# A fused attention and mixture-of-experts kernel: attention's transposes done together, as 64-row halves

## The chip, the cores and the metric

The kernel runs on one core of a Trainium2 chip. A core has a matrix engine (PE, with its weight loads shown apart as PEld), a vector engine (DVE), a scalar engine (ACT), a general engine (POOL) and a queue for transfers (SP). Each engine works through its own instructions in order, and waits on semaphores for the others. In this kernel PE's results go to PSUM tiles, which DVE and ACT read; the text calls 512 float32 of a partition there a bank, the unit in which the program lays these tiles out. The metric is the device time of one launch in microseconds (us), as the median of several runs. Before the change it is 994.02 us (three runs, 993.91 to 994.19).

## The reference

Inputs are x, 16 blocks of 128 tokens by 512 features, and a context of 16 blocks of 128 by 128. There are two residual layers, all in float32:

```
x = x + attention(layernorm(x), context, context)
        # 32 query heads of 16, 8 key/value heads; softmax(q k^T / 4) v per block of 128 tokens
x = x + moe(layernorm(x))
        # gate: sigmoid(x gate_weight^T); 8 groups of 4 experts, best 4 groups, best 8 experts
        # of 32; weights normalized and times 2.5
        # routed: sum over the 8 experts of w2(silu(x w1^T) * (x w3^T)), inner size 256
        # plus one shared expert of the same shape for all tokens
```

## The kernel before

The kernel has three stretches: attention with the gate's inputs (0 to about 134 us), routing with the shared expert (to about 227 us), and the 32 experts (to the end). The program is in order on PE, DVE, ACT and POOL: the order of the calls is the order of the instructions.

**Attention** (`attention_small`) runs over 32 items (b, i): row block b of 128 tokens, and i, which of each pair of key heads. A loop over steps n = 0 to 31 works on three items at once. In step n PE does, in this order: `scores(n)` (L429: four 32-row matmuls side by side, into two PSUM tiles of two banks each, that every step uses again); `values(n-1)` (L445: four matmuls of 32 output columns side by side, into the tile oT); in some steps `gate_parts`, the gate's partial logits; in even steps `queries(n/2+1)`, four 128 by 128 transposes of the normalized rows xq into the tile tr (L416); in some steps `gate_sums` (L505); `added(n-2)`, four transposes of the attention output into the tile o (L461); and in some steps `gate_turn(b)`, four transposes of the rows of the second layernorm into tr (L227).

The other engines follow. ACT takes the two exponentials of `scores` (L439, `p<-sc`) and copies turned rows to xnT (L228). DVE copies oT to oTs (L454) and the turned queries to qT (L420), and for each item takes a reciprocal of the sums (`ri`, L465) and scales the heads (`at`, L467). POOL adds `at` to the residual rows x (L474). Two further chains run through these queues:

- layernorm: DVE's `layernorm_stats` of a block (L91, L92; `mv1` for the first layernorm, `mv2` for the second, which needs both of the block's adds), then `layernorm_rstd`, a chain of 14 small instructions (L98 to L115), on POOL for most groups of blocks (`first_rstd`, `second_rstd`), then `rows_of` (xq, L394, DVE) or `gate_rows` (xn, L217, POOL; it also stores the rows with a transfer on SP). The tile xn has three buffers.
- keys and values: POOL masks the next four blocks' keys (`keys`, kz, L350, two instructions) and copies their values (`values_of`, L357).

Two tables, `head` and `tail`, say which of these are issued at the beginning and at the end of each step; they set the order on DVE and POOL around the adds. Before, in order of the steps: keys 2 at 9; `second_rstd` at 11, 19, 23, 27 (blocks 0-3, 4-7, 8-9, 10-11) and 30 (12-13); `gate_rows` at 13 to 16, 21 to 24, 25, 26, 29, 30; `first_rstd` of blocks 12 to 15 at 16; keys 3 at 17; `mv2` statistics of block b at the end of step 2b + 4, from 4 to 26; squares of the keys (ACT) and their sums (DVE, `kn`) at 17 to 20. Turned rows are in steps 15 to 18, 23 to 28, 30 and 31. Blocks 12 to 15 are done after the loop, between pieces of the shared expert (`filler`).

The program's PSUM tiles in attention take eight banks: four for scores, and one each for tr, lg (the gate), oT and o.

**Experts.** Rows are gathered in slices of 128 (138 in all, L1360), turned on PE by `turn` (up to four slices at a time, each as eight half transposes of 64 rows, two row groups side by side, L1381), and copied to xnT by ACT and DVE in turn (`turned`, L1397 and L1404). All four slices share one PSUM tile of four banks; a slice's two halves lie in two banks, which slices 0 and 1, and slices 2 and 3, share. `up` (L1429) and `down` (L1483) are the experts' matmuls.

Of the kernel before, what the change touches and what calls it, by code (L numbers as in the profile page):

```python
# [18 lines left out]
P = 128  # L19
EPS = 1e-5  # L20
HD = 16
G = 4
# [24 lines left out]
def tile_xattn_moe(  # L47
# [175 lines left out]
    def gate_turn(b, pool, tag="tr", copy=nc.scalar.copy):  # L223
        xn = xn2.pop(b)
        tr = pool.tile([P, ND, P], F32, tag=tag, name="tr")
        for k in range(ND):
            nc.tensor.transpose(tr[:, k, :], xn[:, ts(k, P)], ident)  # L227
        copy(xnT[b // 4][:, :, ts(b % 4, P)], tr)  # L228
# [43 lines left out]
    def attention_small():  # L272


        with ExitStack() as ph:
# [4 lines left out]
            ps_tr = ph.enter_context(tc.tile_pool(name="ps_tr", bufs=1, space=PSUM))  # L280
            ps_lg = ph.enter_context(tc.tile_pool(name="ps_lg", bufs=1, space=PSUM))
            ps_oT = ph.enter_context(tc.tile_pool(name="ps_oT", bufs=1, space=PSUM))
            ps_o = ph.enter_context(tc.tile_pool(name="ps_o", bufs=1, space=PSUM))
# [37 lines left out]
            warm = ps_o.tile([P, P], F32, tag="o", name="warm")  # L321
# [88 lines left out]

            def queries(b):

                xn = xqs.pop(b)
                tr = ps_tr.tile([P, G, P], F32, tag="tr", name="tr")
                for g in range(G):
                    nc.tensor.transpose(  # L416
                        tr[:, g, :], xn[:, g].rearrange("p k d -> p (k d)"), ident
                    )
                qT = ap2.tile([P, G, P], F32, tag="qT", name="qT")
                nc.vector.tensor_copy(qT, tr)  # L420
                qTs[b] = qT

            def scores(b, i):
                scs = [
                    ps_sc.tile([P, 2, G, P], F32, tag="sc", name="sc") for _ in range(NJ // 2)
                ]
                for j in range(NJ):
# [4 lines left out]
                        rhs=qTs[b][rows],  # L432
# [4 lines left out]
                for j, sc in enumerate(scs):  # L437
                    p = pp.tile([P, 2, G, P], F32, tag="p", name="p")
# [3 lines left out]
            def values(b, i):  # L442
                oT = ps_oT.tile([P, G, P], F32, tag="oT", name="oT")
# [10 lines left out]
                nc.vector.tensor_copy(t, oT)  # L454
                oTs[b, i] = t

            def added(b, i):
                t = oTs.pop((b, i))
                o = ps_o.tile([P, G, NJ, HP], F32, tag="o", name="o")
                for g in range(G):  # L460
                    nc.tensor.transpose(  # L461
                        o[:, g].rearrange("p j e -> p (j e)"), t[:, g, :], ident
                    )
                ri = ap2.tile([P, G, NJ], F32, tag="ri", name="ri")
                nc.vector.reciprocal(ri, o[:, :, :, HD])  # L465
                at = ap2.tile([P, G, NJ, HD], F32, tag="at", name="at")
# [3 lines left out]
                    ri.unsqueeze(3).to_broadcast([P, G, NJ, HD]),  # L470
                    ALU.mult,
                )
                part = xs[b].rearrange("p (j i g d) -> p i g j d", i=2, g=G, d=HD)[:, i]
                nc.gpsimd.tensor_tensor(part, part, at, ALU.add)  # L474

# [75 lines left out]

            turned, parts, sums = {}, {}, {}
            at_head(4, fold_of)
            step = 0
            for first, n in ((0, 4), (4, 4), (8, 2), (10, 2)):
                for b in range(first, first + n):
                    at_tail(2 * b + 4, layernorm_stats, b, mv2)
                done = 2 * (first + n - 1) + 4
                at_head(done + 1, second_rstd, first, n, nc.gpsimd)
                for b in range(first, first + n):  # L560
                    step = max(step + 1, done + 3)
                    at_head(step, gate_rows, b, nc.gpsimd)
                    turned[step + (2 if b < 10 else 1)] = b
                    if b % 2 and b < 10:
                        parts[step + 3], sums[step + 4] = b - 1, b - 1
# [5 lines left out]
            queries(0)  # L571
            keep_warm(FILL[-1])
            for n in range(N):
# [4 lines left out]
                if n == 1:  # L578
                    queries(1)
# [1037 lines left out]
```

## Time and profile before

| | |
|---|---|
| median of the runs | 994.02 us |
| the profiled execution's own time | 1000.94 us |
| its span, from the first to the last instruction | 998.9 us |
| granted PE clock, mean | 0.993 |
| busy: PE, PEld, DVE, ACT, POOL | 976.1, 555.6, 300.3, 286.0, 508.5 us |
| scores of step 0 start; step 31 ends | 9.63 us; 119.76 us |
| last matmul of the gate (L505) starts | 133.26 us |
| first gathered slice turned (L1381) | 227.16 us |

Times inside the profiled execution count from the start of its span. A timeline line gives start, length, engine, source line, operation, what is written from what, shapes, how many are merged, and in brackets how long the engine stood idle before and what released it. "PE busy" holds modelled ends, so a wait shorter than a matmul's length may not show as idle. A line of busy times by stretch gives the stretch, its length, and for each engine its busy time and, in brackets, the number of instructions; then the PE clock granted, the share of the transfer engines, and GB/s.

### The profile page before, as it was taken

What the parts mean: (1) busy time and instruction counts of PE and PEld (TensorE: products, weight loads), DVE (VectorE), ACT (ScalarE), POOL (GpSimd) and SP (SyncE); (2) the same over time, 40 slices, a digit from 0 to 9 for tenths busy, and PEclk for the clock granted to TensorE, in tenths of its full rate; (3) what the DMA queues carried; (4) which work ended last, traced back from release to release, by engine and by line L of the source; (5) the groups of instructions that cost most, each with busy time, mean ns of one, the idle gap of its engine ahead of it and who ended that gap; (6) DMA issues with size and microseconds to landing.
All of it is one profiled execution on the core that took longest, in us unless ns stands there. A gap on an engine that the chain in (4) does not pass through costs nothing.

```text
span 998.9 us, 13416 instructions
## 1 busy us (share of the span) xinstructions
PE 976.1 (98%) x4729; PEld 555.6 (56%) x4729; DVE 300.3 (30%) x984; ACT 286.0 (29%) x443; POOL 508.5 (51%) x659
## 2 busy tenths in 40 slices
PE   9999999998999999999999999999999999999996
PEld 5344444546666556676666666667654444444453
DVE  7787678961211112111112111111111111211110
ACT  5567622411222222222222222222222222221221
POOL 3788733752445536444546454545464444455443
PEclk9999999998999999999999999999999999999998
DMA  9011105133767657667767676777576777677543
GB/s 316 4 44 43 63 24 197 46 117 118 171 136 168 142 128 184 150 146 181 162 147 164 155 161 155 161 166 182 131 172 150 150 176 185 141 158 170 116 67 45
DMA packets 59867, 137.12 MB, mean 137 GB/s; under 512 B 12168, under 2 KB 16392, under 8 KB 59792
## 3 DMA queue, kind: packets, MB, share of 16 engines
q0 software_dynamic: 32032, 69.25, 37.0%
q1 hardware_dynamic: 27680, 66.81, 19.9%
q8 instruction: 39, 0.64, 0.3%
q14 instruction: 36, 0.29, 0.1%
q10 hardware_dynamic: 80, 0.13, 0.0%
HBM read 96.71 MB, written 46.73 MB: 144 GB/s over the span
## 4 chain that ended last, share of the span: by engine, by line
PE 77%; POOL 9%; issue 5%; DVE 4%; DMA 2%; another core or an unknown queue 1%; ACT 0%; POOLq 0%; DVEq 0%; ACTq 0%
PE gu L1429 43%; PE y L1483 21%; PE gu L253 5%; PE trx L1381 4%; POOL out_dram L1455 2%; DMA out_dram<-yw,token 2%; POOL xn L217 2%; PE y L1279 1%; POOL x L474 1%; DVE st L91 1%; PE tok L946 1%; POOL kz L350 1%; DVE oTs L454 1%; POOL h L113 0%
## 5 line engine op out<-in xcount | busy, mean ns | idle before, releaser
L1429 PE MATMUL gu<-xnT,wup 128*128 128x256 f32 (+27 forms) x1664 | 493.6, 447 | 4.4 <-DVE xnT L1397 4.4
L1429 PEld LDWEIGHTS gu<-xnT,wup 128*128 128x128 f32 x1664 | 316.4, 191 | 197.9 <-issue 133.5
L1455 POOL DMA_INDIRECT out_dram<-yw,token x150 | 234.7, 1565 | 352.5 <-ACT yw L1492 241.2
L1483 PE MATMUL y<-wdn,sa 128*128 128x512 f32 (+2 forms) x672 | 263.5, 599 | 0.1
L1440 DVE TENSOR_TENSOR sa<-sl,gu 128x256 f32<-128x256 f32 (+27 forms) x104 | 52.2, 502 | 561.9 <-PE gu L1429 519.1
L1360 POOL DMA_INDIRECT xg<-rows,token x138 | 141.9, 1028 | 49.9 <-issue 33.1
L1492 ACT ACTIVATE yw<-y,wt 128x512 f32<-128x512 f32 x138 | 95.0, 688 | 197.7 <-PE y L1483 193.7
L1483 PEld LDWEIGHTS y<-wdn,sa 128*128 128x128 f32 (+2 forms) x672 | 97.9, 170 | 95.1 <-issue 84.6
L1438 ACT ACTIVATE sl<-gu 128x256 f32<-128x256 f32 (+27 forms) x104 | 46.7, 449 | 233.3 <-PE gu L1429 226.9
L1397 ACT COPY xnT<-trx 128x512 f32<-128x512 f32 x65 | 38.1, 586 | 158.4 <-PE trx L1381 67.9
L439 ACT ACTIVATE p<-sc 128x1024 f32<-128x1024 f32 x64 | 62.1, 1022 | 30.2 <-PE sc L429 30.2
L1397 DVE COPY xnT<-trx 128x512 f32<-128x512 f32 x61 | 42.2, 691 | 65.7 <-issue 33.2
L253 PE MATMUL gu<-xnT,sup 128*128 128x512 f32 x128 | 59.2, 601 | 0.7 <-ACT ssl L261 0.7
L940 POOL TENSOR_SCALAR hq<-slice_q,sq 128x138 f16<-128x138 f16 x32 | 35.2, 1114 | 34.7 <-DVE sq L1245 18.5
L1381 PEld LDWEIGHTS trx<-ident,xg 64*128 64x128 f32 x1104 | 37.2, 139 | 17.8 <-issue 17.5
L1381 PE MATMUL trx<-ident,xg 64*128 64x64 f32 x1104 | 42.1, 226 | 0.0
L429 PE MATMUL sc<-qT,kz 32*128 32x512 f32 x256 | 41.5, 639 | 0.2 <-ACT p L439 0.2
L474 POOL TENSOR_TENSOR x<-x,at 128x256 f32<-128x256 f32 x32 | 23.4, 733 | 26.3 <-DVE at L467 26.3
L445 PE MATMUL oT<-p,va 128*32 128x512 f32 x256 | 34.1, 605 | 2.5 <-DVE oTs L454 2.5
L253 PEld LDWEIGHTS gu<-xnT,sup 128*128 128x128 f32 x128 | 22.8, 190 | 24.1 <-issue 21.5
L1412 DVE SCALAR_TENSOR_TENSOR own<-expert,owner,xg 128x32 f32<-128x32 f32 x138 | 31.5, 245 | 0.0
L1279 PE MATMUL y<-sdn,sa 128*128 128x512 f32 x64 | 29.3, 595 | 0.0
(180 smaller groups left out, 494.0 us busy)
## 6 DMA issues: line engine op xcount, KB each, us to landing
wup<-in_w_dram SPq DMA_DIRECT2D x64, 512.0 KB
wdn<-in_w_dram SPq DMA_DIRECT2D x32, 512.0 KB
rows<-xn SPq DMA_DIRECT2D x16, 256.0 KB
out_dram<-x SPq DMA_DIRECT2D x16, 256.0 KB
x<-in_x_dram SPq DMA_DIRECT2D x15, 256.0 KB
out_dram<-yw,token POOLq DMA_INDIRECT x150
xg<-rows,token POOLq DMA_INDIRECT x138
cTs<-in_cT_dram SPq DMA_DIRECT2D x4, 256.0 KB
```

What stands on the lines that cost most here:

```text
L253: nc.tensor.matmul(acc, lhsT=sup[:, w, d, ts(i, P)], rhs=xnT[k][:, d, :], start=(d == 0), stop=(d == ND - 1),)
L429: nc.tensor.matmul(scs[j // 2][:, j % 2], lhsT=kzs[b // 4 % 2][rows, b % 4, i, :], rhs=qTs[b][rows], start=True, stop=True, tile_position= ...
L439: nc.scalar.activation(p, sc, AF.Exp, scale=1.0 / HD**0.5)
L1360: nc.gpsimd.indirect_dma_start(out=t, out_offset=None, in_=rows[:, :], in_offset=bass.IndirectOffsetOnAxis(ap=token[:, j : j + 1], axis=0) ...
L1381: nc.tensor.matmul(tr[:, h, s, d, :], lhsT=xg[j][rows_of_half, ts(d, P)], rhs=ident[rows_of_half, rows_of_half], start=True, stop=True, is ...
L1397: copy(xnT[n % NTB][:, :, col : col + P].rearrange("p d (h t) -> p h d t", h=2), tr)
L1429: nc.tensor.matmul(acc[:, 0:m], lhsT=wup[k % NW][:, w, d, ts(i, P)], rhs=xnT[n % NTB][:, d, 0:m], start=(d == 0), stop=(d == ND - 1),)
L1438: nc.scalar.activation(banks[2][:, 0:m], acc[:, 0:m], AF.Silu)
L1440: nc.vector.tensor_tensor(acts[n % NTB][:, i, 0:m], banks[2][:, 0:m], acc[:, 0:m], ALU.mult)
L1455: ins = nc.gpsimd.indirect_dma_start(out=flat, out_offset=bass.IndirectOffsetOnAxis(ap=token2[:, k - 1 : k] if a else token[0:b, j : j + 1 ...
L1483: nc.tensor.matmul(y[c0:c1, :], lhsT=acts[n % NTB][:, i, col : col + c1 - c0], rhs=wdn[pieces[n][0] % NW][:, i, :], start=(i == 0), stop=( ...
L1492: nc.scalar.activation(yws[j], y, AF.Copy, scale=wt[:, j : j + 1])
```

## The change

In attention, the sets of four 128-row transposes of one step (queries, added heads, turned rows) are issued one after the other by a new function `transposes`, at the place in the step where queries stood, behind `gate_parts` and ahead of `gate_sums`. Each 128 by 128 transpose becomes two of 64 rows in PE's two row groups: eight half transposes a set. A step has at most two sets. They go into one PSUM tile x of two banks, one bank for each row group, both sets in both banks; only when all have been issued do the readers follow (qT, then `ri` and `at`, then the copy of the turned rows, which stays on ACT). The tiles tr and o go, so x has their two banks. The layouts of qT, oTs, `at` and the residual add change with the halves.

The order of the gate's work changes: `second_rstd` of blocks 0-2, 3-5, 6-8, 9-11 at steps 9, 15, 21, 27; `gate_rows` at 10, 12, 14 and so on to 26 for blocks 0 to 8, then 28, 29, 30; turned rows three steps later, in odd steps 13 to 29, then 30 and 31, and block 11 after the loop; `gate_parts` at 16, 20, 24, 28 and 31. Blocks 12 to 15 and the last heads are still turned as full transposes, in a tile with the same tag.

In the experts, `turn` uses two PSUM tiles of two slices each instead of one of four (the same four banks); ACT copies the first two slices and DVE the last two.

```diff
-    def gate_turn(b, pool, tag="tr", copy=nc.scalar.copy):
+    def gate_turn(b, tr, copy=nc.scalar.copy):
         xn = xn2.pop(b)
-        tr = pool.tile([P, ND, P], F32, tag=tag, name="tr")
         for k in range(ND):
             nc.tensor.transpose(tr[:, k, :], xn[:, ts(k, P)], ident)
         copy(xnT[b // 4][:, :, ts(b % 4, P)], tr)
...
-            ps_tr = ph.enter_context(tc.tile_pool(name="ps_tr", bufs=1, space=PSUM))
+            ps_x = ph.enter_context(tc.tile_pool(name="ps_x", bufs=1, space=PSUM))
             ps_lg = ph.enter_context(tc.tile_pool(name="ps_lg", bufs=1, space=PSUM))
             ps_oT = ph.enter_context(tc.tile_pool(name="ps_oT", bufs=1, space=PSUM))
-            ps_o = ph.enter_context(tc.tile_pool(name="ps_o", bufs=1, space=PSUM))
...
+            H = P // 2
+            halves = [slice(h * H, (h + 1) * H) for h in range(2)]
+            def transposes(*sets):
+                x = ps_x.tile([P, 2, 2, 2, P], F32, tag="x", name="x")
+                for s, (of, split, _) in enumerate(sets):
+                    for k in range(4):
+                        for h, rows in enumerate(halves):
+                            if split:
+                                to = x[:, h, :, s, ts(k, P // 4)]
+                                by = ident[rows, rows].rearrange("p (a b) -> p a b", a=2)
+                            else:
+                                to = x[:, h, k // 2, s, ts(k % 2, H)]
+                                by = ident[rows, rows]
+                            nc.tensor.matmul(
+                                to,
+                                lhsT=of[rows, k, :],
+                                rhs=by,
+                                start=True,
+                                stop=True,
+                                is_transpose=True,
+                                tile_position=(h * H, 0),
+                            )
+                for s, (_, _, then) in enumerate(sets):
+                    then(x[:, :, :, s])
             def queries(b):
-                xn = xqs.pop(b)
-                tr = ps_tr.tile([P, G, P], F32, tag="tr", name="tr")
-                for g in range(G):
-                    nc.tensor.transpose(
-                        tr[:, g, :], xn[:, g].rearrange("p k d -> p (k d)"), ident
-                    )
-                qT = ap2.tile([P, G, P], F32, tag="qT", name="qT")
-                nc.vector.tensor_copy(qT, tr)
-                qTs[b] = qT
+                xn = xqs.pop(b).rearrange("p g k d -> p g (k d)")
+                def then(x):
+                    qTs[b] = ap2.tile([P, 2, 2, P], F32, tag="qT", name="qT")
+                    nc.vector.tensor_copy(qTs[b], x)
+                return xn, False, then
...
+                nc.vector.tensor_copy(
+                    t.rearrange("p g (h s) -> p h g s", h=2),
+                    oT.rearrange("p (h g s) -> p h g s", h=2, g=G),
+                )
                 oTs[b, i] = t
...
-            def added(b, i):
-                t = oTs.pop((b, i))
-                o = ps_o.tile([P, G, NJ, HP], F32, tag="o", name="o")
-                for g in range(G):
-                    nc.tensor.transpose(
-                        o[:, g].rearrange("p j e -> p (j e)"), t[:, g, :], ident
-                    )
-                ri = ap2.tile([P, G, NJ], F32, tag="ri", name="ri")
+            def add(b, i, o):
+                ri = ap2.tile([P, NJ, G], F32, tag="ri", name="ri")
                 nc.vector.reciprocal(ri, o[:, :, :, HD])
-                at = ap2.tile([P, G, NJ, HD], F32, tag="at", name="at")
+                at = ap2.tile([P, NJ, G, HD], F32, tag="at", name="at")
                 nc.vector.tensor_tensor(
                     at,
                     o[:, :, :, 0:HD],
-                    ri.unsqueeze(3).to_broadcast([P, G, NJ, HD]),
+                    ri.unsqueeze(3).to_broadcast([P, NJ, G, HD]),
                     ALU.mult,
                 )
-                part = xs[b].rearrange("p (j i g d) -> p i g j d", i=2, g=G, d=HD)[:, i]
+                part = xs[b].rearrange("p (j i g d) -> p i j g d", i=2, g=G, d=HD)[:, i]
                 nc.gpsimd.tensor_tensor(part, part, at, ALU.add)
+            def added(b, i):
+                return (
+                    oTs.pop((b, i)),
+                    True,
+                    lambda x: add(b, i, x.rearrange("p h r (g e) -> p (h r) g e", e=HP)),
+                )
+            def turn_of(b):
+                def then(x):
+                    nc.scalar.copy(
+                        xnT[b // 4][:, :, ts(b % 4, P)].rearrange(
+                            "p (r k) (h s) -> p h r k s", r=2, h=2
+                        ),
+                        x.rearrange("p h r (k s) -> p h r k s", k=2),
+                    )
+                return xn2.pop(b).rearrange("p (k d) -> p k d", d=P), False, then
...
-            step = 0
-            for first, n in ((0, 4), (4, 4), (8, 2), (10, 2)):
-                for b in range(first, first + n):
+            for first in range(0, 12, 3):
+                for b in range(first, first + 3):
                     at_tail(2 * b + 4, layernorm_stats, b, mv2)
-                done = 2 * (first + n - 1) + 4
-                at_head(done + 1, second_rstd, first, n, nc.gpsimd)
-                for b in range(first, first + n):
-                    step = max(step + 1, done + 3)
-                    at_head(step, gate_rows, b, nc.gpsimd)
-                    turned[step + (2 if b < 10 else 1)] = b
-                    if b % 2 and b < 10:
-                        parts[step + 3], sums[step + 4] = b - 1, b - 1
+                at_head(2 * first + 9, second_rstd, first, 3, nc.gpsimd)
+            for b in range(11):
+                n = min(2 * b + 13, b + 21)
+                turned[n] = b
+                at_head(max(n - 3, b + 19 if b > 8 else 0), gate_rows, b, nc.gpsimd)
+            at_head(30, gate_rows, 11, nc.gpsimd)
+            for b in range(0, 8, 2):
+                parts[2 * b + 16], sums[2 * b + 17] = b, b
+            parts[31] = 8
             at_tail(28, layernorm_stats, 12, mv2)
...
                 if n > 0:
                     values(*items[n - 1])
                 if n in parts:
                     gate_parts(parts[n])
+                sets = []
                 if n % 2 == 0 and 0 < n // 2 < B - 1:
-                    queries(n // 2 + 1)
+                    sets.append(queries(n // 2 + 1))
+                if n > 1:
+                    sets.append(added(*items[n - 2]))
+                if n in turned:
+                    sets.append(turn_of(turned[n]))
+                if sets:
+                    transposes(*sets)
                 keep_warm(FILL.get(n, 0))
                 if n in sums:
                     gate_sums(sums[n])
-                if n > 1:
-                    added(*items[n - 2])
-                if n in turned:
-                    gate_turn(turned[n], ps_tr)
...
-            added(*items[N - 2])
+            transposes(added(*items[N - 2]), turn_of(11))
             values(*items[N - 1])
+            gate_sums(8)
             gate_rows(13, nc.vector)
-            gate_turn(12, ps_tr)
-            added(*items[N - 1])
-            gate_turn(13, ps_tr)
+            both = ps_x.tile([P, 2, ND, P], F32, tag="x", name="tr")
+            tr, o = both[:, 0], both[:, 1]
+            gate_turn(12, tr)
+            last = oTs.pop(items[N - 1])
+            for g in range(G):
+                nc.tensor.transpose(o[:, g], last[:, g, :], ident)
+            add(*items[N - 1], o.rearrange("p g (j e) -> p j g e", e=HP))
+            gate_turn(13, tr)
...
-        ps_x = ctx.enter_context(tc.tile_pool(name="ps_x", bufs=1, space=PSUM))
+        ps_x = ctx.enter_context(tc.tile_pool(name="ps_x", bufs=2, space=PSUM))
...
-            tr = ps_x.tile([P, 2, NX, ND, H], F32, tag="trx", name="trx")
+            trs = [
+                ps_x.tile([P, 2, 2, ND, H], F32, tag="trx", name="trx")
+                for _ in range(-(-len(js) // 2))
+            ]
...
-                            tr[:, h, s, d, :],
+                            trs[s // 2][:, h, s % 2, d, :],
...
-                turned(j, tr[:, :, s], (nc.scalar.copy, nc.vector.tensor_copy)[s % 2])
+                turned(j, trs[s // 2][:, :, s % 2], (nc.scalar.copy, nc.vector.tensor_copy)[s // 2])
```

## The prediction

> **What bounds the kernel now.** I read the page first (engine shares, slices), then PE's waits, then busy time by stretch, then the timelines of 34 to 62 us and 300 to 306 us.
>
> ```profile
> PE 976.1 (98%) x4729; PEld 555.6 (56%) x4729; DVE 300.3 (30%) x984; ACT 286.0 (29%) x443; POOL 508.5 (51%) x659
> PE gu L1429 <- DVE xnT L1397: 4.4, 1, 4.4
> ```
>
> PE fills 98% of the span; from 232 us on (the experts) its one long wait is 4.4 us at the first expert. Only attention, up to about 134 us, can give or lose much. By stretch (us, then busy PE, PEld, DVE, ACT, POOL):
>
> ```profile
> 35.00:55.00 20.00, 18.84 (x134) 7.49 (x132) 15.14 (x36) 11.56 (x12) 14.75 (x38) 1.00 0.01 2
> 55.00:75.00 20.00, 18.58 (x148) 8.56 (x144) 16.56 (x38) 13.43 (x19) 16.31 (x25) 1.00 0.15 54
> 75.00:95.00 20.00, 19.52 (x153) 8.69 (x153) 15.23 (x36) 13.89 (x17) 16.60 (x38) 1.00 0.11 41
> ```
>
> PE looks full, but DVE and POOL stand at 75 to 83%, in order, each waiting for the other. The reader is to see that PE's cover is thin. The timeline of POOL, then of DVE, around steps 9 to 11 (start, length):
>
> ```profile
> 42.77 0.72 POOL L474 TENSOR_TENSOR x<-x,at 128x256 f32<-128x256 f32 x1
> 43.47 3.12 POOL L350 TENSOR_SCALAR kz<-cTs,odd 128x512 f32<-128x512 f32 x2
> 46.55 0.73 POOL L474 TENSOR_TENSOR x<-x,at 128x256 f32<-128x256 f32 x1
> 48.61 0.28 POOL L98 TENSOR_SCALAR ve<-mv 128x4 f32<-128x4 f32 x1
> 52.34 0.20 POOL L115 TENSOR_TENSOR rstd<-h,r 128x4 f32<-128x4 f32 x1
> 53.89 2.08 POOL L217 TENSOR_SCALAR xn<-x,mv,rstd 128x512 f32<-128x512 f32 x1
> ```
>
> ```profile
> 46.27 0.42 DVE L467 TENSOR_TENSOR at<-o,ri 128x256 f32<-128x256 f32 x1
> 47.32 0.69 DVE L91 BATCH_NORM_STATS2 st<-x 128x6 f32<-128x512 f32 x1 [0.63 <-POOL x L474]
> 48.15 0.66 DVE L394 TENSOR_SCALAR xq<-x,mv,rstd 128x512 f32<-128x512 f32 x1
> 48.73 0.68 DVE L454 COPY oTs<-oT 128x512 f32<-128x512 f32 x1
> ```
>
> DVE's statistics of row block 3 (47.32) start 0.04 us after POOL's add of step 9 lands (46.55 + 0.73). The rstd chain of the second layernorm (48.61 to 52.54, 3.9 us, step 11) comes after it. Last, transposes in both forms, and the copies behind them:
>
> ```profile
> 50.88 0.66 PE L416 MATMUL tr<-ident,xq 128*128 128x128 f32 x4
> 51.37 0.60 PE L461 MATMUL o<-ident,oTs 128*128 128x128 f32 x4
> 51.90 0.31 PEld L429 LDWEIGHTS sc<-qT,kz 32*128 32x128 f32 x8 [0.17 <-issue]
> 302.41 1.21 PE L1381 MATMUL trx<-ident,xg 64*128 64x64 f32 x32
> 303.67 0.59 ACT L1397 COPY xnT<-trx 128x512 f32<-128x512 f32 x1 [2.24 <-PE trx L1381]
> 304.28 0.69 DVE L1397 COPY xnT<-trx 128x512 f32<-128x512 f32 x1 [1.12 <-issue]
> ```
>
> A set of four full transposes holds PE 0.49 us (50.88 to 51.37). Four sets as halves hold it from 302.41 to 303.55, where the next matmul starts: 0.285 a set. ACT's and DVE's copies from one tile go one after the other.
>
> **1. PE work removed.** 59 sets become halves: 16 of queries, 31 of `added`, 12 of turned rows. In attention the neighbours are 32-row and 32-column matmuls, which no row shows next to halves; bounds 0.25 and 0.49 (no gain), taken 0.30, near the expert row with one entry. So 59 x 0.19 = 11.2 us less PE work. [...]
>
> How much reaches the step? Call S(n) the start of step n's scores; before: S10 41.95, S11 45.60, S12 48.25. Scores take 1.07 us, values 1.00. Both score tiles are reused each step, so the second half of scores(n+1) waits for the second exp(n), which ends 3.2 us after S(n). The row at 45.60 shows it: exps run from 46.83 to 48.77, the held-back half starts at 48.82. Hence a pair of steps costs 3.22 + 1.07 + 1.0 + the transposes of the even step: 5.29 + 1.02 = 6.31, as measured (6.30). With 0.6 for two sets as halves it is 5.9: 0.4 us a pair, not 0.8, since ACT takes over.
>
> Up to step 8 DVE is back to back (33.7 to 38 us) and hides most of it: with the saved transposes on the path (0.3 us by step 2, two shorter sets before S9) S10 comes about 0.9 us early, POOL's add of step 7 0.3 us early.
>
> **2. rstd chain from step 11 to step 9, behind the keys and ahead of step 9's add.** The program as built has on POOL: add 8, kz x2, rstd chain, add 9. POOL is busy without a gap from add 7 on, so add 9 lands at 46.6 - 0.3 + 3.9 + 0.73 = 50.9, not 47.28. DVE's statistics of block 3 wait for it, and behind them in DVE's queue stand xq (0.6), the oT copy (0.68) and step 11's reciprocal and `at`. DVE, free at 46.0, sits idle 4.9 us. PE then waits: values(11) needs oT free, 50.97 + 0.82 + 0.61 + 0.68 = 53.1; plus 1.0 and 0.63, S13 = 54.8 against 51.90, so **+2.9 us**. Of the 4.9 us, 2.0 are PE's own lead there (0.9 at S10, 1.1 that scores and values run ahead).
>
> **3. Steps 13 to 21: more POOL work, and a copy tied to DVE.** Through step 18 the new order puts on POOL one rstd chain (3.9) and one gate-row pass (2.08) more than before. From the statistics of step 14 (63.3) POOL runs rstd 3.9, add 0.7, rstd1 3.9, gate rows 2.1, add 0.7, kz 3.1: add 17 starts at 77.8, against 74.79 before. **+3.0** at 21 steps, no gain from PE. A new wait: added heads and turned rows now share two banks, so ACT's copy of turned rows waits for DVE's `at`; before it started 0.11 us after the transpose. Behind it in ACT's queue stand the next two exps (1.94) and sq. Where DVE is late (steps 13, 15, 19) exps start 0.9 to 2.3 us later than the scores allow; in step 20 to 21 that costs 1.8 us more: S22 about +4.7. Bounds: 0 (DVE early) and 1.3 a turn (DVE row chain 0.68 + 0.25 + 0.42). As to why it must wait: the 303.67 and 304.28 rows show it here. [...]
>
> **4. Steps 22 to 31: the gain.** POOL has slack, and each odd step has one turn instead of bursts. Before, steps 22 to 26 took 18.6 us (83.68 to 102.29): turns of 0.55, gate parts 0.55, sums 0.37, and waits for gate rows (0.59 in step 24). Now steps 22 and 23 cost 5.95, steps 24 and 25 7.0 (with parts 0.43, sums 0.37 and 0.25 for late exps), step 26 2.7: 15.65 us. S27 is at +4.7 - 3.0 = +1.7.
>
> **5. The end.** Before, after step 26's statistics POOL did rstd, add, add, gate rows, add, gate rows, rstd: 104.09 to 120.71, 16.6 us, waits for `at` among them. Now it does rstd 3.9, three gate rows 6.2, three adds 2.1, rstd 3.9 = 16.1 without a gap, from 106.25 (S27 at 104.0, then qT 0.7, reciprocal and `at` 0.7, statistics 0.8). So the last rstd ends at 122.4: **+1.7**, however far PE catches up by then. DVE's gate rows 12 wait for it, and behind them the last heads. In the epilogue the joint set waits for the joint tile, where three tiles stood: turn 12 for ACT's copy of turn 11 behind DVE's `at`, **+0.7** (bounds 0 and 1.3, the chain of part 3).
>
> **6. Experts.** Two tiles let ACT and DVE copy side by side; copies end 1.3 us earlier but PE waits for neither (303.55 to 305.37 is `down`). At the first expert both copies go on ACT: 2 x 0.59 for 0.62 + 0.69: **-0.1**. PE's 11.2 us are covered by nothing here.
>
> Costed at nothing: oT's copy in new order and turned rows' copy (0.69 and 0.59 in that form at L1397), row stores on SP (3.4 us to land, buffer reused two turns later or after its turn). POOL's add has longer runs: 0.73 taken; bounds 0.26 (its memset, 1.02 ns an element) and 1.04 (gate rows, 4.06), some -1.9 to +1.2 on the last chain.
>
> **Sum:** +1.7 + 0.7 - 0.1 = +2.3 us. The profiled execution took 1000.94 (span 998.9): 1003.2 (1001.2). It stands 6.9 above the median, 994.02; carried over unscaled: **996.3**.
>
> **Rivals.** *A, faster:* DVE's backlog of steps 6 to 8 dissolves. POOL sat idle 3.3 us before add 7 (37.92), waiting for `at`; if PE's shorter sets bring that `at` forward by 3.3, add 9 lands near 47.6 and DVE hardly waits. It decides from a lead of some 3 us at add 7 on (I count 0.3). Then the 2.9 are gone and PE keeps its 0.9 of S10 and 0.6 more to S13: -4.4, 991.9; with adds at 0.26, 990. Against it: DVE was back to back there with statistics that don't move. *B, nothing:* ACT's copy costs no exp time (DVE early): -1.8 in step 21 and the same in the end: 994.5. For it: DVE is only 75% busy. *C, worse:* POOL and DVE get in each other's way more: xq took 0.52 to 1.08 us, the slow ones beside gate rows; ten slow ones on DVE's path give +3 to +5: 999.3 to 1001.3. *D, halves don't pay here:* the pair stays 6.3; from S22 five pairs, +0.4 each, 998.3.
>
> **Chances.** Forecast 0.48 (own range 995 to 998.5; 0.35 of it over the bound of 0.2%, 2.0 us, which is what a measurement of this kernel can tell), A 0.25, B 0.14, C 0.08, D 0.05. Slower 0.48, same 0.27, faster 0.25. Leaving out half of C and some of A, the range is 991.3 to 999.3.
>
> **What would show it.** Right: a DVE wait of 4 to 5 us on POOL's add near 46 to 51 us; values(11) late; exps behind turned copies; POOL without gaps from 106 to 122; a half set at 0.30. Wrong: DVE st of block 3 before 48 us, pairs of 6.3 after step 22, or a last rstd that ends before 120. What would break it all is a price of POOL's add or chain that the new order changes.

## The result, and the profile after

The changed kernel takes **1004.19 us** (1003.41 to 1005.45, 4 runs) against 993.96 (993.79 to 994.19, 4 runs): 1.0102 times as long, 95% interval 1.009 to 1.0115. In two more series the ratio was 1.0094 (1.0077 to 1.0111) and 1.0097 (1.0081 to 1.0114). The forecast was +2.3 us, 996.3, with 999.3 as its upper end: the sign was right, the size was not.

The page of the profile after (1003.76 us, span 1002.0), its engines, and the group of the experts' first matmuls with PE's wait at its end:

```profile
PE 972.2 (97%) x4965; PEld 550.7 (55%) x4965; DVE 294.2 (29%) x983; ACT 285.2 (28%) x444; POOL 507.9 (51%) x659
...
L1483 PE MATMUL gu<-xnT,wup 128*128 128x256 f32 (+27 forms) x1664 | 490.6, 445 | 1.2 <-ACT xnT L1451 1.2
```

At the first expert PE waits 1.2 us here and 4.4 in the profile of before, which also ran at half clock for 6.83 us after it. That is no part of the change: in three of the four series of runs below every kernel, the one before included, has the longer wait (the kernel before then takes 999.4 to 999.8 instead of 994), and in the other one none has. So times are compared within a series only, and for the path inside attention I use a pair from the series without it: the changed kernel again (span 999.3) and the kernel before with the experts' tiles (span 991.9, same time as before).

Busy time in two stretches, the second one around the last step; its row of before stands last (the columns are PE, PEld, DVE, ACT, POOL, then the granted clock, DMA share and GB/s):

```profile
35.00:55.00 20.00, 14.20 (x130) 4.84 (x129) 11.24 (x27) 9.56 (x10) 15.43 (x38) 0.94 0.04 14
115.00:135.00 20.00, 16.66 (x129) 7.92 (x129) 8.39 (x21) 9.41 (x14) 10.84 (x22) 0.74 0.18 66
115.00:135.00 20.00, 18.46 (x121) 9.60 (x118) 12.37 (x38) 9.53 (x16) 8.52 (x21) 1.00 0.18 66
```

PE is busy for 14.2 us of the first stretch where it was for 18.8, and the clock column, 1.00 in both stretches before, drops to 0.94 there and to 0.74 after the last step. In the same order as in the prediction, POOL, then DVE, then PE at steps 9 to 12:

```profile
42.80 3.11 POOL L348 TENSOR_SCALAR kz<-cTs,odd 128x512 f32<-128x512 f32 x2
46.00 0.24 POOL L98 TENSOR_SCALAR ve<-mv 128x3 f32<-128x3 f32 x1
...
49.63 0.19 POOL L115 TENSOR_TENSOR rstd<-h,r 128x3 f32<-128x3 f32 x1
49.79 0.72 POOL L497 TENSOR_TENSOR x<-x,at 128x256 f32<-128x256 f32 x1
```

```profile
45.22 0.42 DVE L490 TENSOR_TENSOR at<-x,ri 128x256 f32<-128x256 f32 x1
50.54 0.69 DVE L91 BATCH_NORM_STATS2 st<-x 128x6 f32<-128x512 f32 x1 [4.90 <-POOL x L497]
...
51.37 0.73 DVE L392 TENSOR_SCALAR xq<-x,mv,rstd 128x512 f32<-128x512 f32 x1
52.02 0.68 DVE L479 COPY oTs<-oT 128x512 f32<-128x512 f32 x1
```

```profile
46.60 1.89 PE L454 MATMUL sc<-qT,kz 32*128 32x512 f32 x8
52.75 1.94 PE L470 MATMUL oT<-p,va 128*32 128x512 f32 x8 [4.25 <-DVE oTs L479]
54.62 0.69 PE L427 MATMUL x<-ident,xq 64*128 64x64 f32 x8
55.10 0.64 PE L427 MATMUL x<-ident,oTs 64*128 64x64 f32 x8
55.66 1.26 PE L454 MATMUL sc<-qT,kz 32*128 32x512 f32 x8
```

This is part 2 as forecast: the chain (46.00 to 49.82) ahead of the add, DVE idle 4.90 us (4.9 in the forecast), behind it xq and the copy of oT, and PE idle for 4.25. But then the values take 1.94 us where 1.07 is usual, and the transposes 0.48 and 0.56 from start to start instead of 0.30: PE's clock is halved from 52.55 to 55.96. S13, the start of step 13's scores, comes at 55.66 instead of the forecast 54.8.

After the last step, again PE:

```profile
123.65 0.47 PE L427 MATMUL x<-ident,oTs 64*128 64x64 f32 x8 [1.48 <-ACT xnT L508]
...
124.31 1.93 PE L470 MATMUL oT<-p,va 128*32 128x512 f32 x8
...
127.05 1.09 PE L226 MATMUL tr<-ident,xn 128*128 128x128 f32 x4
128.82 1.12 PE L661 MATMUL tr<-ident,oTs 128*128 128x128 f32 x4 [0.68 <-ACT xnT L227]
130.88 1.11 PE L226 MATMUL tr<-ident,xn 128*128 128x128 f32 x4 [0.95 <-DVE at L490]
```

The last pair of half sets waits 1.48 us for ACT's copy of the rows before it. Then the last heads (128.82) and the turn of block 13 (130.88) each wait for a reader of the joint tile; the turn of block 12 shows no wait here, in the pair 0.47 us. All of it from 124.22 to 134.46 runs at half clock. Where the time goes, in the pair (start of a step's scores and later points, us):

| | before | changed | difference | forecast |
|---|---|---|---|---|
| S13 | 51.69 | 56.00 | +4.3 | +2.9 |
| S22 | 83.45 | 90.27 | +6.8 | +4.7 |
| S27 | 102.06 | 105.85 | +3.8 | +1.7 |
| end of POOL's last chain | 120.46 | 124.51 | +4.1 | +1.7 |
| gate's last logits | 133.38 | 140.74 | +7.4 | +2.4 |
| end of the span | 991.9 | 999.3 | +7.4 | +2.3 |

From the last logits on the difference stays 7.4. This profiled execution, 1001.40, has no half clock after the last step; the three others of that series take 1003.4 to 1003.7 at a mean clock of 0.990 to 0.991 instead of 0.995. So the loss is 7.4 us, and some 2 more in most executions.

### The profile page after: what moved, and what is told of

It is laid out like the page before. It is cut to its first block, busy times and chain, and to the rows that moved or that the text cites. A ratio compares the mean times of both kernels' runs of the same rounds, so it can differ in the third digit from the quotient of the medians.

```text
span 1002.0 us, 13955 instructions
## 1 busy us (share of the span) xinstructions
PE 972.2 (97%) x4965; PEld 550.7 (55%) x4965; DVE 294.2 (29%) x983; ACT 285.2 (28%) x444; POOL 507.9 (51%) x659
## 4 chain that ended last, share of the span: by engine, by line
PE 79%; DVE 5%; POOL 5%; issue 5%; DMA 3%; ACT 1%; POOLq 0%; DVEq 0%; ACTq 0%
PE gu L1483 42%; PE y L1537 21%; PE gu L252 5%; PE trx L1435 4%; POOL out_dram L1509 3%; PE y L1330 2%; DMA out_dram<-yw,token 2%; PE sc L454 2%; PE oT L470 1%; DVE st L91 1%; PE x L427 1%; PE tok L997 1%; DVE oTs L479 1%; POOL kz L348 1%; DVE at L490 0%
## 5 line engine op out<-in xcount | busy, mean ns | idle before, releaser
L1451 ACT COPY xnT<-trx 128x512 f32<-128x512 f32 x69 | 37.2, 589 | 91.5 <-PE trx L1435 91.5
L454 PE MATMUL sc<-qT,kz 32*128 32x512 f32 x256 | 46.5, 642 | 0.5 <-ACT p L464 0.4
L1435 PEld LDWEIGHTS trx<-ident,xg 64*128 64x128 f32 x1104 | 37.2, 139 | 17.8 <-issue 17.5
L1451 DVE COPY xnT<-trx 128x512 f32<-128x512 f32 x57 | 39.3, 689 | 5.8 <-PE trx L1435 5.1
```

The lines of the kernel that those rows point to most:

```text
L454: nc.tensor.matmul(scs[j // 2][:, j % 2], lhsT=kzs[b // 4 % 2][rows, b % 4, i, :], rhs=qT[rows], start=True, stop=True, tile_position=(j * ...
L1435: nc.tensor.matmul(trs[s // 2][:, h, s % 2, d, :], lhsT=xg[j][rows_of_half, ts(d, P)], rhs=ident[rows_of_half, rows_of_half], start=True, ...
L1451: copy(xnT[n % NTB][:, :, col : col + P].rearrange("p d (h t) -> p h d t", h=2), tr)
```

## The experiments

**The first expert, and what is the same everywhere.** The kernel before, unchanged:

> The kernel before, unchanged. Its profiled execution took 1000.94 us (span 998.9), with PE idle 4.4 us at the first expert and its clock at half for 6.8 us behind that. Theory (baseline): that idle and that half clock are not in its timed executions, some 7 us together; their spans are near 992 and the granted clock nearer 1.0 than 0.993. Rival: the timed executions have the same 999 us span and profiling just adds 7 us; then the 10 us of the change lie where the two profiles differ.

Measured: 999.49 (10 runs) beside 999.75 for the same kernel, and the profile shows the wait at the first expert (4.40 us, half clock for 3.41 us after it). Neither side of the expectation holds as it was put: profile and timed runs agree in this series, with the wait in both, and lie 5.8 us over the first timed runs of the same kernel: that is why only ratios within a series are used here.

Then the changed kernel itself in two other series:

> The changed kernel, unchanged, beside the kernel before on one chip. Where its two-sided cost is real, the ratio of the first pair of runs, 1.010, returns: on this chip the kernel before takes 999.75, so 1010. Where the 1.010 was made by the first expert (in the profile of before PE idles there 4.4 us and then runs at half clock, and in the changed kernel's profile it does not; the timed runs may have it the other way round), the changed kernel takes 1004, 1.004, and the two profiles' difference of 3 us is the true cost.

> The changed kernel again, so that the next ones have it on their own chip: 9 to 10 us over before, with PE's clock halved for some windows of 3.41 us at step 12 in every run and, in most runs, after the last step.

Measured: 1003.48 beside 994.24 (1.0094), and 1009.26 beside 999.65 (1.0097): the ratio returns, as the first of the expectations has it. In the last series every run has a mean clock of 0.988 to 0.989; the profiled one has the half clock at the end. The cost is in attention and the same with and without the long wait at the first expert. And the experts' part alone:

```
-  tr = ps_x.tile([P, 2, NX, ND, H]), bufs=1, one tile for 4 sets
+  trs = [ps_x.tile([P, 2, 2, ND, H]) for each 2 sets], bufs=2
```

> The kernel before with the experts' two PSUM tiles alone. The prediction says -0.1 us, so 999.7. The rival: the changed first expert (both copies on ACT, no copy on DVE behind it) takes away the 4.4 us of idle PE and the half clock after it; then 994 to 996, and the change's attention part costs 4 us more than it seems.

Measured: 993.97 beside 994.24, ratio 0.9999 (0.9989 to 1.0008): part 6 is right, it is worth nothing.

**The chain out of DVE's way.** The second layernorm's chains behind the add of their step instead of ahead of it; alone, and with the last heads in a tile of their own:

```
-  at_head(2 * first + 9, second_rstd, first, 3, nc.gpsimd)
+  at_tail(2 * first + 9, second_rstd, first, 3, nc.gpsimd)
```

> The changed kernel with second_rstd of blocks 0 to 11 at the end of steps 9, 15, 21, 27 instead of the beginning, so behind that step's residual add on POOL. Theory (order): DVE's wait of 4.9 us for add 9 falls under 1 us, PE's idle of 4.25 us in step 12 goes and with it the half clock of 3.4 us; 4 to 5 us faster than the changed kernel at step 13, of which POOL's full stretch of steps 14 to 20 may take back 1 to 2: 1000 to 1002 us. Rival (the copies of turned rows behind DVE are the cost): step 22 starts no earlier than before this edit, 1003 to 1005 us.

> Both edits. Theory: the two losses are apart and add up, 7 to 10 us faster than the changed kernel: 994 to 997 us, about the kernel before. Rival (half transposes or ACT copies behind DVE are slow in themselves): not below 1000 us.

Measured: 1012.32 (1.0143, 1.0118 to 1.0168) and 1008.86 (1.0092, 1.0075 to 1.0108): even after the 5.8 us that this series' kernel before takes more, some 5 and some 7 us over what was expected. By its ratio the first is slower than the changed kernel (1.0094 to 1.0102 in its three series), the second no better. Step 12 is repaired, S13 comes at 51.68 and 51.62. But the chain of step 15 now stands in POOL's queue right ahead of the chain of the next queries, gate rows and keys. POOL, then DVE, in the first run (chains of small steps left out):

```profile
69.48 0.20 POOL L115 TENSOR_TENSOR rstd<-h,r 128x3 f32<-128x3 f32 x1
...
73.40 0.20 POOL L115 TENSOR_TENSOR rstd<-h,r 128x4 f32<-128x4 f32 x1
73.58 2.08 POOL L217 TENSOR_SCALAR xn<-x,mv,rstd 128x512 f32<-128x512 f32 x1
75.63 0.73 POOL L497 TENSOR_TENSOR x<-x,at 128x256 f32<-128x256 f32 x1
76.36 3.11 POOL L348 TENSOR_SCALAR kz<-cTs,odd 128x512 f32<-128x512 f32 x2
79.42 0.72 POOL L497 TENSOR_TENSOR x<-x,at 128x256 f32<-128x256 f32 x1
```

```profile
76.40 0.42 DVE L490 TENSOR_TENSOR at<-x,ri 128x256 f32<-128x256 f32 x1 [1.96 <-POOL x L497]
80.18 0.69 DVE L91 BATCH_NORM_STATS2 st<-x 128x6 f32<-128x512 f32 x1 [3.35 <-POOL x L497]
```

POOL works from 65.56 to 80.1 without a gap, two adds are late, PE idles 4.22 us at 78.8 and then runs at half clock for 6.83 us; S22 is at 91.39. The stall was moved, not removed.

Next, the chains off POOL altogether:

```
-  at_head(2 * first + 9, second_rstd, first, 3, nc.gpsimd)
+  at_tail(2 * first + 8, second_rstd, first, 3)          # on DVE
```

> The changed kernel with the five chains of the second layernorm on DVE (2.2 us each by the rows at 10.61 to 12.74) instead of POOL (3.9), right behind the statistics they need. Where POOL's queue is the cause of parts 2, 3 and 5, DVE's wait of 4.9 us for the add of step 9 goes, S13 is at 52 to 53, S22 at 84 to 86, the last chain ends before 120 instead of at 124, and the kernel gains 5 to 8 us on the changed one. Where DVE, 75% busy, can't carry 2.2 us more, S13 is past 54 and the gain under 2 us.

Measured: 1008.18 beside 994.24 (1.0141, 1.0124 to 1.0158), 4.7 slower than the changed kernel: the rival's side. The wait for the add is gone, but the chain, beside POOL's add and keys (42.41 to 46.2), took 3.4 us instead of 2.2, and the copy of oT stands behind it:

```profile
42.55 0.61 DVE L100 TENSOR_SCALAR r<-ve 128x3 int32<-128x3 int32 x1
43.20 0.62 DVE L108 SCALAR_TENSOR_TENSOR h<-r 128x3 f32<-128x3 f32 x1
43.86 0.16 DVE L109 TENSOR_TENSOR h<-h,ve 128x3 f32<-128x3 f32 x1
```

S13 56.26, S22 94.01; this execution also has half-clock windows at 37.2, 47.4 and 95.2 us. Neither queue took the chain here for nothing.

**Order or layout?** The kernel before with the new order of chains and gate rows alone (full transposes, old tiles), and the complement: halves for queries and heads with the old order, turned rows as full sets in the bank of the gate's parts, a tile for each set after the last step.

```
 (first, on before)
+  for first in range(0, 12, 3): ... at_head(2*first + 9, second_rstd, first, 3, nc.gpsimd)
+  turned[min(2*b + 13, b + 21)] = b
 (second, on the changed kernel)
+  for first, n in ((0, 4), (4, 4), (8, 2), (10, 2)): ...            # as before
+  gate_turn(turned[n], ps_lg.tile([P, TB], tag="lg"))
```

> The kernel before (full transposes, a PSUM tile for each kind of set) with the new order of the second layernorm's chains and gate rows alone. If that order is the cause of parts 2, 3 and 5 (a chain ahead of the add of step 9; a full POOL; the last chain late), DVE waits 4 to 5 us for the add of step 9, S13 is at 54.5 to 56 as in the changed kernel (before 51.7), the last chain ends 3 to 4 us late, and with no joint tile at the end the time is 4 to 6 us over before: 998 to 1000. If the halves and shared banks are the cause, it stays within 1 us of before, 994 to 995.

> The complement: the changed kernel with the old order of chains and gate rows; queries and added heads as joint halves, turned rows as full sets in the bank of the gate's parts, and at the end a tile for each set. If the order is the cause, no long wait for the add of step 9, S13 at 51 to 52, the last chain at 119 to 121, and 992 to 996 in all, so that the halves alone are worth between -2 and +2 us. If sharing banks is the cause, it is past 998.

Measured beside 999.42: the order alone 1004.52 (1.0052, 1.0035 to 1.0068), the halves with the old order 1001.99 (1.002, 1.001 to 1.003). In the first, DVE, then PE:

```profile
50.89 0.69 DVE L91 BATCH_NORM_STATS2 st<-x 128x6 f32<-128x512 f32 x1 [4.52 <-POOL x L474]
```

```profile
53.10 1.93 PE L445 MATMUL oT<-p,va 128*32 128x512 f32 x8 [3.48 <-DVE oTs L454]
54.96 1.12 PE L416 MATMUL tr<-ident,xq 128*128 128x128 f32 x4
```

The order alone makes the same stall, with the same half clock behind it: S13 56.59, S22 90.80, the last chain ends at 125.50. So the order is the cause of part 2 and of the late last chain in part 5. Of part 3 it is not shown to be the whole cause. ACT in step 20, first in the pair's changed kernel, then in the run with the order alone:

```profile
83.36 0.59 ACT L508 COPY xnT<-x 128x512 f32<-128x512 f32 x1 [3.75 <-DVE at L490]
84.38 1.93 ACT L464 ACTIVATE p<-sc 128x1024 f32<-128x1024 f32 x2
```

```profile
82.99 1.92 ACT L439 ACTIVATE p<-sc 128x1024 f32<-128x1024 f32 x2
```

With the joint tile the copy of turned rows stands behind `at`, and the exps behind the copy: they start 5.2 us after POOL's add 17 (79.14), with the order alone 3.5 us after it (79.53). From S13 to S22 both kernels take 34.2 to 34.3 us all the same, but the run with the order alone has another half-clock window (83.56 to 86.97), in which values to next scores take 4.08 us instead of 2.74.

With the old order S13 is at 50.59, S22 at 83.61. That run's +2.6, outside the -2 to +2 expected, came from the bank that I shared: in steps 18, 26 and 28 the turn waits for DVE's copy of the gate's sums.

```profile
71.99 0.63 PE L546 MATMUL lg<-fold,lgTs 128*128 128x32 f32 x4
73.77 0.63 PE L226 MATMUL tr<-ident,xn 128*128 128x128 f32 x4 [1.14 <-DVE logits L549]
```

With the sums moved ahead of the transposes these waits go:

```
+  if n in sums: gate_sums(sums[n])
   if sets: transposes(*sets)
-  if n in sums: gate_sums(sums[n])
```

> Halves with the old order and, in steps 18, 20, 26, 28 and 30, the gate's sums ahead of the transposes, so that a turn in the same bank finds it copied. The run without this had three waits of 1.14 us there, step 31 2.5 us later than before, and 2.6 us in all over before. If those waits are the whole of it, 1 to 2 us under before; if PE's saved work is covered by ACT, DVE and POOL anyway, within 1 us of before.

Measured: **998.44** beside 999.65, ratio 0.9984 (0.9975 to 0.9994). S13 50.63, S22 83.30, last logits 132.24 against 133.38 to 133.49 of before. This is the one version of attention that beats both kernels, by 1.2 us, inside the 0.2% that I called no change. It has 47 half sets, its turned rows being full sets: by the forecast's 0.19 us a set that is 8.9 us less transposing on PE, and 1.2 us is what it is worth.

**The half clock.** Matmuls of zeros in PE's idle time of step 12 of the changed kernel:

```
+  if n == 12: keep_warm(17)
   if n > 0: values(*items[n - 1])
```

> The changed kernel with 17 matmuls of zeros in PE's idle time of step 12 (about 3.8 of its 4.25 us), which nobody waits for. Where the half clock after that idle time is what puts S13 0.9 us later than forecast, the clock stays whole up to the epilogue, S13 comes at 54.2 to 54.8 instead of 55.66, and the end 1 us earlier if steps 13 to 21 pass it on. Where POOL alone sets steps 13 to 21, S13 moves and S22 stays at 89.8, and the time stays.

Measured: 1002.98 beside 994.24 (1.009, 1.0073 to 1.0107), 0.5 less than the changed kernel in that series, with overlapping intervals. PE:

```profile
48.92 4.06 PE L323 MATMUL warm<-wz 128*128 128x128 f32 x34
53.24 1.07 PE L470 MATMUL oT<-p,va 128*32 128x512 f32 x8 [0.27 <-DVE oTs L479]
54.24 0.46 PE L427 MATMUL x<-ident,xq 64*128 64x64 f32 x8
```

The values take 1.07 again, no half clock before 123 us, S13 is at 54.88, 1.1 earlier, where the prediction had it (54.8); S22 and the last chain come 0.9 and 1.0 us earlier. The half clock at step 12 is shown, at 1 us. In the time it hardly shows; what happens after the last step may hide it (this profile has two half-clock windows there, the pair's none).

After the last step, three runs: the last heads in a tile of their own; then a tile for each set; then that, with two pieces of the shared expert's matmuls moved forward into PE's waits.

```
-  both = ps_x.tile([P, 2, ND, P]); tr, o = both[:, 0], both[:, 1]
+  gate_turn(12, bank(ps_sc)); o = ps_oT.tile([P, TB]); gate_turn(13, bank(ps_x))
+  gate_turn(15, bank(ps_x)); gate_turn(14, bank(ps_sc), nc.vector.tensor_copy)
 (third)
+  filler(1)
   transposes(added(*items[N - 2]), turn_of(11))
+  filler(1)   # ahead of the turn of block 12
```

> The changed kernel with the last heads (item 31) turned into a PSUM tile of their own (from oT's pool) instead of the second bank of the tile that the last turned rows use. Theory (joint tile): the chain turn 12, ACT copy, heads 31, DVE at, turn 13 falls apart, PE's waits of 0.7 and 0.95 us go, and if the half clock of 10.2 us from 124 us on comes from PE's thin work there it gets shorter: 2 to 6 us faster, 998 to 1002 us. Rival: the end is set by POOL's last rstd chain (122.4 us forecast, 123.8 us measured) and nothing is won, 1004 us.

> The changed kernel with a tile for each set after the last step. In the changed kernel's profile on this chip the gate's last logits come 15.9 us after the end of the last chain, before 12.6. If the 3.3 us are waits that are built for the whole joint tile (turn of block 12, last heads, turns of 13 and 14), they come down to 12.5 to 13.5 and the kernel to 1000 to 1001.5. If the half clock there is what costs, the times stay at 1003 wherever it comes.

> The same with two pieces of the shared expert's matmuls (1.0 us each) moved from the end into PE's idle time before the last heads, which also keeps PE busy there. If the half clock follows from idle PE, no half clock between 115 and 135 us in the profile and 1.5 to 2.5 us less than with the tiles alone where that has it; if not, the same time as the tiles alone, within 0.5.

Measured: 1005.03 beside 999.75 (1.0051, 1.0035 to 1.0068); 1003.58 beside 999.42 (1.004, 1.0026 to 1.0054); 1003.38 (1.0039, 1.0024 to 1.0053). The first is some 4 to 5 us below the changed kernel by the ratios, and 2 to 6 were expected; in its profile turn, heads and turn follow each other too, but at half clock (124.51 to 131.34). The second, PE after the last chain's end at 125.37:

```profile
127.15 0.63 PE L226 MATMUL tr<-ident,xn 128*128 128x128 f32 x4
127.68 0.66 PE L664 MATMUL o<-ident,oTs 128*128 128x128 f32 x4
128.36 0.63 PE L226 MATMUL tr<-ident,xn 128*128 128x128 f32 x4
128.92 0.64 PE L531 MATMUL lgT<-xnT,gw 128*32 128x256 f32 x8
```

Turn, heads and turn follow each other without a wait, and from the end of the last chain to the last logits it is 13.0 us (before 12.9, changed kernel 16.2 without and 18.9 and 19.5 with half clock). So the joint tile's waits cost **3.2 us**. With them gone the profile has no half clock there, so the third run says nothing of the filler and the clock; it does say that moving the work alone wins nothing (0.2 us, inside the intervals). The filler with the joint tile left as it is, one piece more ahead of the turn of block 13:

> The changed kernel with its joint tile at the end left, and three pieces of the shared expert (1.0 us of matmuls each) moved forward into PE's waits there. If the half clock after the last step comes from PE idling between short transposes, it goes, and the kernel is 1.5 to 2.5 us faster than the changed one; if the tile's waits cost all of it, it stays within 0.5 of the changed one.

Measured: 1006.11 beside 1009.26 for the changed kernel in the same series, **-3.2 us**. Busy time in the changed kernel, in the 3.41 us ahead of its half clock and in the half clock; then in this run, over about the same work:

```profile
126.42:129.83 3.41, 2.02 (x16) 1.36 (x12) 1.77 (x5) 1.17 (x2) 1.05 (x2) 1.00 0.42 154
...
129.83:136.65 6.82, 6.13 (x20) 2.94 (x20) 2.48 (x8) 2.45 (x4) 0.72 (x1) 0.50 0.01 2
```

```profile
122.60:126.00 3.40, 2.97 (x33) 1.16 (x29) 1.92 (x5) 1.54 (x3) 2.82 (x10) 1.00 0.00 0
126.00:129.50 3.50, 2.82 (x15) 1.84 (x16) 1.61 (x5) 1.17 (x2) 0.91 (x2) 1.00 0.41 151
```

With PE busy for 81 to 87% instead of 59% the clock stays whole (1.00 instead of 0.50). From S31 to the last logits it is 22.6 us instead of 24.9, though three pieces of 1.0 us more stand ahead of them; two of the joint tile's waits are still there (0.68 us each), filler stands in the others. So 2.3 us are the half clock's. In these two profiles 0.6 us more came ahead of S31 (S22 90.38 against 90.99), where the half clock of step 12 is one window instead of two; the medians' 3.2 is not split further.

**Does it add up?** All remedies at once (zeros in step 12, a tile for each set, filled waits):

> The changed kernel with all three remedies: matmuls of zeros in step 12, a tile for each set and filled waits at the end. What is left of the loss is then the order of chains and gate rows. By the sum: the 9.2 less 1.1 (half clock of step 12), 3.3 (tile waits) and 2.1 (half clock of the end): 2.5 to 3.5 us over before. If the causes overlap, 4 or more, as with the tiles alone.

Measured: 1002.86 beside 999.65, **+3.2 us** (1.0032, 1.002 to 1.0045), inside the range that the sum gives. The changed kernel in that series is at +9.6; 6.4 are the clock's and the joint tile's, 3.2 are left for the order net of the 1 us that the halves give.

## Why the prediction was wrong

- **Part 1, right.** Half sets start 0.30 us apart (the lower bound of 0.25, half of a full set's 0.49, was an estimate), pairs after step 22 take 5.93 us (forecast 5.95), and the saved work hardly reaches the path: 1.2 us of 8.9 in the best version. In that version PE waits 5.1 us for DVE's copy of oT, seven times, where it waited 2.5 us, three times, before.
- **Part 2, right in mechanism, short by a term.** DVE idle 4.90 us, forecast 4.9; S13 +4.3 instead of +2.9. It had "**+2.9 us**" from the waits alone (its terms add to 54.7, +2.8). What failed is that no step asked what PE's clock does after 4 us of idle time: 1.1 us, shown by the zeros in step 12. The profile of before had the price in it, at the first expert: 4.4 us of idle, then 6.83 us at half clock.
- **Part 3, both reasons seen, 0.7 us short.** In the pair's changed kernel POOL works from 64.58 to the end of the keys without a gap and add 17 starts at 79.14, 14.6 us later (14.5 in the forecast). The exps behind ACT's copy start 1.8 us later after that add than with the order alone. From S13 to S22 the forecast had 33.6 us; measured are 34.3 (34.0 to 35.0 in all runs with the changed kernel's order and joint sets), before 31.8. How much of it the copy costs by S22 is open: the order alone takes 34.2 without that copy, but with a half-clock window and longer transposes in its place.
- **Part 4, right.** Steps 22 to 26: 15.58 us, forecast 15.65. With the order alone it is 16.46 (before 18.61), so 2.15 of the 3.0 regained are the spread-out turns', 0.9 the joint halves'.
- **Part 5, the step that failed most.** The last chain runs 16.25 us without a gap (forecast 16.1), only later, by what parts 2 and 3 lacked. But "turn 12 for ACT's copy of turn 11 behind DVE's `at`, **+0.7**" counted one wait on the joint tile where four were built: the turn of 12 for the readers of the pair before it, then the last heads, the turn of 13 and the turn of 14, each for the reader of the *other* half of the tile. They cost 3.2 us. And its upper bound, 1.3, was the bound of one of them. The half clock of this stretch, 2.3 to 3.2 us in the profiles that have it, had no step: in the profile after it follows on the window with the 1.48 us wait, in the last series on a window with three of the four waits.
- **Part 6, right** as far as the runs can tell: 0.9999.
- **Costed at nothing.** The row stores' "3.4 us to land" is a timeline row of two issues (56.00 to 59.38); in the profile after a store lands 2.0 us after its issue (median).
- **The sum.** At the last logits +2.4 became +7.4: 1.0 (half clock of step 12), 0.7 (steps 13 to 21), 2.6 (three more waits on the joint tile) and 0.7 that was not traced; with the half clock of the end the median is at +9.2. "Carried over unscaled" did no harm: the long wait at the first expert, which the profiled execution had, comes or stays away in both kernels alike.
- **Rivals.** A: DVE did wait its 4.9 us. B: its premise, that ACT's copy costs no exp time, is not what the rows of step 20 show. C: its range came nearest, by a mechanism that the runs didn't show. D: halves pay, if little.

## What to carry to other kernels

Price a stall twice: once as the wait, and once as the half clock behind it, where the runs show one (here 4.25 us of idle in step 12, and 1.0 us for the half clock); look in the profile of before for a place where it already happened, and read the clock column there. Before tiles are merged, list every pair of writer and reader that then shares one, since here each was a wait for the whole tile, a reader of its other half included (0.68 us for the last heads, 0.95 for the turn of block 13, 3.2 for all after the last step), and count the waits, not the tiles. And where PE only filled the time that DVE, ACT and POOL left, as in attention here, some 9 us less of PE's work were worth 1, and the order in which a slow queue gets its work cost 5, two half-clock windows included.

## What the runs showed of the hardware

- **The half clock came in windows of 3.41 us.** In the profile after, PE's granted clock changes at 52.55, 55.96, 124.22 and 134.46 us: 3.41, 68.27 and 10.24 us apart, which is 1, 20 and 3 times 3.413. At the first expert of before it is halved from 231.53 to 238.35, twice that. Every half-clock stretch between 10 and 225 us, in 18 profiles, lasts 3.41 us or a multiple of it. With 17 of them cut into such windows (the other has no half clock to set the cut by) and counted by PE's busy share, half clock followed on none of 924 full-clock windows over 0.75, on 1 of 49 between 0.6 and 0.75, on 9 of 28 between 0.5 and 0.6, and on 15 of 16 below. So the executions of one kernel differ, and no single share divides them: at the end the changed kernel kept its clock after a window of 0.56 and lost it after 0.54 and after 0.59. After the last step the longest gap in the profile after was 1.48 us and the clock was halved all the same, so here the busy share of the window tells more than the longest gap.
- **Half sets alone thinned PE's work out.** Around 33 to 38 us the emptiest 3.41 us have PE busy for a share of 0.53 in the kernels with half sets and of 0.64 to 0.65 without, and 5 of the 14 profiles with half sets run at half clock from 36 or 37 us on, the others not. S10 is then later (42.2 to 42.7 against 40.7 to 41.3); in the two of them that have the changed kernel's order nothing of it is left at S22 (89.7 and 89.8, the others 89.3 to 91.2).
- **The same kernel differs by 5.5 us between series of runs.** The kernel before has a median of 994.0 and 994.2 in two, 999.4 to 999.8 in three. In the longer ones ACT's first copy of turned rows starts 3.0 us after the transposes, PE idles 4.0 to 4.4 us instead of 1.17, and half clock follows (6.83 us in the first profile of before, 3.41 us when it ran again). The trace names no instruction as the releaser; this was not resolved.
- **Three small DVE operations took three times as long beside the start of a POOL operation.** In the run with chains on DVE three of the eleven operations of the chain at 42.35 took 0.54 to 0.62 us instead of 0.16. Each started 0.07 to 0.16 us after an add or a key mask had started on POOL and ended 0.69 to 0.75 us after that start; the others took 0.16 to 0.17 beside the same keys. The cause is not shown.
